# Re-dealing the steps of two low-rank MLPs around an eight-sequence encoder, inside one large single-core kernel

## The chip, the cores and the metric

The kernel runs on one core of a Trainium2 chip. Four engines matter here, each with its own queue that it works through in order: PE (TensorE, the matrix engine), DVE (VectorE), ACT (ScalarE) and POOL (GpSimd). A fifth queue, SP, issues most of the DMA transfers. The metric is the time of one execution on the device in microseconds (us), lower is better; the median of three executions is quoted.

## The reference, cut to what matters

The network adds eight sublayers to a residual stream `x` of shape (8, 256, 128), each on a layer-normed input. The first four are a linear recurrence, a low-rank-modulated MLP, a four-layer encoder, and the same MLP a second time:

```python
x = L0_attn_a_u
x = x + _L0_attn_a_ref(_layernorm(x, axis=-1), ...)      # recurrence
x = x + _L0_ffn_ref(_layernorm(x, axis=-1), ...)         # low-rank MLP, first time
x = x + _L0_attn_b_ref(_layernorm(x, axis=-1), ...)      # encoder, 4 layers
x = x + _L0_ffn_ref(_layernorm(x, axis=-1), ...)         # low-rank MLP, second time
x = x + _L1_attn_a_ref(_layernorm(x, axis=-1), ...)      # causal attention
...
```

The low-rank MLP and one encoder layer are these:

```python
def _L0_ffn_ref(x, W1, b1, W2, b2, scale):
    lt = x[:, 1:17]; even, odd = lt[:, ::2], lt[:, 1::2]
    m1 = (even[:, :4, :, None] * odd[:, :4, None, :]).reshape(Bx, Hx, Dx)
    m2 = (even[:, 4:, :, None] * odd[:, 4:, None, :]).reshape(Bx, Dx, Hx)
    h = einsum('bsd,hd->bsh', x, W1) + scale * einsum('bsd,bhd->bsh', x, m1) + b1
    h = gelu(h)
    return einsum('bsh,oh->bso', h, W2) + scale * einsum('bsh,boh->bso', h, m2) + b2

def _encoder_layer(x, ...):
    h = _layernorm(x); q, k, v = h @ Wq, h @ Wk, h @ Wv
    x = x + _linear_attention(q, k, v) @ Wo
    h = _layernorm(x)
    return x + relu(h @ W1 + b1) @ W2 + b2
```

(The kernel's program takes the shapes of a larger instance: 8 batches of 512 tokens, D = 128.)

## The kernel before

A batch of 512 tokens lies in SBUF as four tiles of 128 x 128. All work on a batch is a Python generator that is cut into *steps* by `yield`. `pieces` (line 35) deals such generators out in rounds: its list of *ages* is one round, and the slot of age `a` in round `now` advances generator `now - a` by one step. A generator therefore starts in an early round at its lowest age and ends at its highest. A slot that has no generator (at the start and the end) does nothing but still counts, so `pieces` can advance a second stream, `side`, at every `every`-th slot from round `first` on. `in_program_order` (line 65) then pins the instructions of PE, DVE, ACT and POOL to the order in which they were written: what is dealt first stands first in each engine's queue.

**The low-rank MLP** is `lora_steps` (line 331). Per batch, in the order of its steps: layer-norm statistics (L174, L175, L160 on DVE, then the power -1/2 on POOL, L161); the normed tile `z` (two quarters on DVE, L192, two on ACT, L188) and a bias added into `x` on POOL (L221); transposes on PE (L201) and four small row picks (L358), evacuated to `zt`; `left` and `e` on DVE (L364 to L375); two outer-product matmuls (L381) and `w1e`, `w2e` on DVE (L384, L385); the up matmuls (L391) with Gelu on ACT (L392), in two steps; the down matmuls (L399), in two steps, and the add into `x` (L224). The first MLP is followed by two steps of `encoder_input` (statistics; normed and scaled on ACT, L188, four instructions, with a POOL add, L424). The second one is preceded by two steps of `encoder_output` (statistics; four ACT instructions, L188, then three POOL operations on 128 x 512, L439 to L441).

**The encoder** is `encoder_block` (line 479). 32 generators (4 layers x 8 batches) of 15 steps go through 35 rounds (-1 to 33) of 15 slots. In the order of its steps: 0 statistics; 1 normed `hn`; 2 bias add on POOL (L221); 3 transposes (L201) and `zt` (L208); 4 key, value and query matmuls (L533, L536), `vx` copies (L538) and two exponentials (L542, L547) on ACT, `kb` and `kp` on DVE (L540, L543); 5 L553, then `qp`, `ks`, `kv` on DVE (L555 to L560); 6 L567, then `den`, `at` on DVE (L569 to L571); 7 transposes (L581) and the copy `att` (L583); 8 output projection (L475), add (L586), statistics; 9 `hn`; 10 transposes and `zt`; 11 and 12 up matmuls (L600) with Relu (L601), step 11 with a POOL bias add (L221); 13 and 14 down matmuls (L608) and the add (L613). Gelu and the exponential are in different ACT tables, so that ACT loads a table (1.28 us in the trace) whenever it goes from one to the other.

How the three are joined. At the front, `before` (line 2250) deals the recurrence, the first MLP beside it, and beside the last rounds of that MLP the encoder's first pieces: `side=take(side, 22), every=1, first=B - 2`, one encoder piece after each slot of the MLP's rounds 6 and 7, 22 in all, and none in its rounds 8 and 9. Two of the 22 are `filled()` (L496 to L502), which sets constants on POOL. At the back, one piece of the second MLP is dealt after each of the encoder's last twelve pieces; the rest runs after the encoder in a region of program order of its own, with a pool of its own (`lora`, two buffers of `mlp_g`). From its round 5 on, the four steps of `attention_input` (two layer norms of batch 0 and a transpose, for the causal attention) stand beside it.

Behind that, `attention_block` clears two tiles `strips0`, `strips1` on POOL (L680, L683), and the weights of the experts (`w_m`, 4.5 MB) are loaded by SP into the room of the encoder's weights once these are free.

Of the kernel before, what the change touches and what calls it, by code (L numbers as in the profile page):

```python
# [10 lines left out]
F32 = mybir.dt.float32  # L11
# [8 lines left out]
P = 128  # L20
B = 8
S = 512
# [14 lines left out]
def pieces(make, count, ages, side=None, every=0, first=0):  # L37

    live = {}
    done = 0
    starts = {start: n for n, start in enumerate(range(count) if isinstance(count, int) else count)}
    for now in range(min(ages), 1 + max(starts) + max(ages)):
        for age in ages:
            n = starts.get(now - age)
            if n is not None:
                if n not in live:
                    live[n] = make(n)  # L50
                next(live[n], None)
            done += 1
            if side is not None and now >= first and done % every == 0:
                next(side, None)
            if n is not None:
                yield
# [271 lines left out]
LORA_FIRST = (2, -2, 0, 1, -1, 0, 2, -1, 1, -1, -2)  # L328
LORA_SECOND = (-3, -2, 0, 1, -1, 0, -1, 1, -1, -2, -4)


def lora_steps(k, room, ahead=None, behind=None):

    nc = k.nc
    w, pool = k.packs["f"], k.work

    def steps(b):
        if ahead is not None:  # L340
            for _ in ahead(b):
                yield
        x = k.xb(b)
        found = k.norm_start(x)
        yield
        z = k.work.tile([P, NT, D], F32, name="z")
        k.norm_end(x, z, found, split=True)
        k.add_bias(x, k.row["f_b2"])
        yield

        zt = k.work.tile([P, S], F32, name="zt")
        k.flip(z, zt)


        pt = k.ps([P, 2, D], "b")
        for g in range(4):
            rows = slice(32 * (g % 2), 32 * (g % 2) + 4)
            nc.tensor.matmul(pt[rows, g // 2, :], w["pick"][0:32, g, :], z[0:32, 0, :], start=True, stop=True)  # L358
        yield
        left = pool.tile([P, D], F32, name="left", bufs=1)  # L360
        e = pool.tile([P, 4, D], F32, name="e", bufs=1)
        parts = [slice(32 * i, 32 * i + 4) for i in range(2)]
        for rows in parts:
            nc.vector.tensor_scalar(left[rows], pt[rows, 0, :], k.col["scale"][rows, :], None, ALU.mult)  # L364
        one, two = parts
        nc.vector.tensor_tensor(
            e[one],
            pt[one, 1:2, :].to_broadcast([4, 4, D]),
            k.ident[one, one, None].to_broadcast([4, 4, D]),
            ALU.mult,  # L370
        )
        e2 = e[two].rearrange("p c (i q) -> p c i q", i=4)
        ev = pt[two, 1, :].rearrange("p (q c) -> p c q", c=4)
        for i in range(4):
            nc.vector.tensor_scalar(e2[:, :, i, :], ev, k.ident[two, 32 + i : 33 + i], None, ALU.mult)  # L375
        yield
        w1 = pool.tile([P, 512], F32, name="w1e")
        w2 = pool.tile([P, 4, D], F32, name="w2e")
        p1, p2 = k.ps([P, 512]), k.ps([P, 4, D])
        for rows, to in ((one, p1), (two, p2.rearrange("p c o -> p (c o)"))):  # L380
            nc.tensor.matmul(  # L381
                to, left[rows], e[rows].rearrange("p i d -> p (i d)"), start=True, stop=True
            )
        nc.vector.tensor_tensor(w1, w["w1"], p1, ALU.add)  # L384
        nc.vector.tensor_tensor(w2, w["w2"], p2, ALU.add)  # L385
        yield

        g = room().tile([P, 4, S], F32, name="mlp_g")
        for c in range(4):
            ph = k.ps([P, S])  # L390
            nc.tensor.matmul(ph, w1[:, c * P : (c + 1) * P], zt, start=True, stop=True)  # L391
            nc.scalar.activation(g[:, c, :], ph, AF.Gelu, bias=k.col["f_b1"][:, c : c + 1])  # L392
            if c % 2:
                yield

        py = k.ps([P, NT, D], "c")
        for t in range(NT):
            for c in range(4):
                nc.tensor.matmul(  # L399
                    py[:, t, :], g[:, c, t * P : (t + 1) * P], w2[:, c, :], start=(c == 0), stop=(c == 3)  # L400
                )
            if t == 1:
                yield
        k.add_x(b, py)
        yield
        if behind is not None:
            for _ in behind(b):
                yield

    return steps  # L410


def encoder_input(k, xe):

    nc = k.nc

    def steps(b):
        xb = xe[:, b * NT : (b + 1) * NT, :]
        mean, rs = k.norm_start(k.xb(b))
        yield  # L420
        scaled = k.small.tile([P, NT], F32, name="ln_sc")
        nc.vector.tensor_scalar(scaled, rs, math.sqrt(D), None, ALU.mult)
        k.norm_end(k.xb(b), xb, (mean, scaled), split=2)
        nc.gpsimd.tensor_tensor(xb, xb, k.packs["e"]["pos"], ALU.add)  # L424
        yield

    return steps


def encoder_output(k, xe):  # L430

    nc = k.nc

    def steps(b):
        xb = xe[:, b * NT : (b + 1) * NT, :]
        found = k.norm_start(xb)
        yield
        k.norm_end(xb, xb, found, split=2)
        nc.gpsimd.tensor_tensor(xb, xb, k.lnf[:, 0:1, :].to_broadcast([P, NT, D]), ALU.mult)  # L439
        nc.gpsimd.tensor_tensor(xb, xb, k.lnf[:, 1:2, :].to_broadcast([P, NT, D]), ALU.add)  # L440
        nc.gpsimd.tensor_tensor(k.xb(b), k.xb(b), xb, ALU.add)  # L441
        yield

    return steps
# [34 lines left out]
def encoder_block(k, xe, before, behind):  # L479
# [3 lines left out]
    nc, tc = k.nc, k.tc  # L483
# [3 lines left out]
    with tc.tile_pool(name="enc1", bufs=1, reuse_waits="tile") as one, tc.tile_pool(name="enc", bufs=2, reuse_waits="tile") as pool:  # L487
# [134 lines left out]
        left = L * B * len(ages)  # L622
        own = chain(filled(), pieces(steps, L * B, ages))
        with in_program_order(tc):

            done = 0

            def counted():
                nonlocal done
                for _ in own:  # L630
                    done += 1
                    yield

            stream = counted()
            before(pool, stream)
            for _ in stream:
                if done > left + 2 - 12:
                    next(behind)


def attention_input(k, b, pool, to, **bufs):

    x = k.xb(b)
    found = k.norm_start(x)
    yield
    z = pool.tile([P, NT, D], F32, name="z", **bufs)
    k.norm_end(x, z, found)
    found = k.norm_start(z)
    yield
    hn = pool.tile([P, NT, D], F32, name="hn", **bufs)  # L650
    k.norm_end(z, hn, found)
    yield
    k.flip(hn, to, k.col["l_ln1s"], k.col["l_ln1b"])
    yield
# [367 lines left out]
class Experts:  # L1022
# [37 lines left out]
    def behind(self, made):  # L1060
        tc = self.k.tc
        for i in reversed(tc.nc.cur_bb.bb.instructions):
            if i.engine == mybir.EngineType.PE:
                tc.add_manual_dep(made.ins, i.name, SYNC, reason="not all of them at once")
                return
# [356 lines left out]
def run(stream):  # L1422
    for _ in stream:
        pass
# [16 lines left out]
def take(stream, many):  # L1441

    for _ in range(many):
        if next(stream, stream) is stream:
            return
        yield
# [749 lines left out]
def net_kernel(ctx: ExitStack, tc: tile.TileContext, drams, offsets, out):  # L2196
    nc = tc.nc
    k = Net(ctx, tc, drams, offsets)
    for b in range(B):
# [20 lines left out]
    room = rooms.enter_context(tc.tile_pool(name="moe1", bufs=1, side="right", reuse_waits="tile"))  # L2220
    p_l = own.enter_context(tc.tile_pool(name="w_l", bufs=1, side="right", reuse_waits="tile"))
    ready = p_l.tile([P, S], F32, name="zt0")
# [11 lines left out]
    slots = [blank_slots(k, one) for one in GROUPS]  # L2234
    k.load("l", p_l, parts=2)
    k.load("lrow", p_l, rows=P)
    second = []
    xe = w_e.enter_context(tc.tile_pool(name="xe", bufs=1, reuse_waits="tile")).tile([P, B * NT, D], F32, name="xe")
    behind = pieces(
        lora_steps(k, lambda: second[0], ahead=encoder_output(k, xe)),  # L2240
        B,
        LORA_SECOND,
        side=attention_input(k, 0, k.work, ready),
        every=2,
        first=5,
    )

    def before(pool, side):
        free = xe.rearrange("p t d -> p (t d)")[:, (B - 2) * S :]
        k.load("a", queue=nc.scalar, into=free)  # L2250
        first = lora_steps(k, lambda: pool, behind=encoder_input(k, xe))
        after = pieces(first, B, LORA_FIRST, side=take(side, 22), every=1, first=B - 2)
        pipeline(rotation_steps(k, pool, free), B, ROTATION, side=after, every=3, first=5)
        run(after)

    with k.banks(**usual):
        encoder_block(k, xe, before, behind)
        with tc.tile_pool(name="lora", bufs=2, reuse_waits="tile") as pool, in_program_order(tc):
            second.append(pool)
            run(behind)  # L2260
    w_e.close()
    late = ctx.enter_context(tc.tile_pool(name="w_m", bufs=1, reuse_waits="tile"))
    rest = ExitStack()
# [262 lines left out]
```

## Time and profile before

| what | value |
|---|---|
| median of three executions | 1931.11 us (1929.14 to 1938.34) |
| the profiled execution's own time | 1931.14 us |
| its span in the profile | 1929.4 us |
| PE busy | 1687.2 us, 87% |
| DVE busy | 1267.0 us, 66% |
| ACT busy | 987.6 us, 51% |
| POOL busy | 766.5 us, 40% |
| recurrence and first MLP | about 0 to 190 us |
| encoder | about 135 to 638 us |
| second MLP | about 610 to 729 us |
| causal attention, experts, gated attention, experts | 729 to 1929 us |

The span is the time from the first to the last instruction that the profiler recorded; the 1.7 us between it and the execution's time lie around it. A row of the timeline gives the start and the length of an instruction (or of a group of equal ones, x count), its engine and source line, what it writes and reads, and in brackets how long its engine had been idle before it and which instruction released it. A row of a table of windows gives for a stretch of the span its length and each engine's busy time (with the number of instructions), then the mean granted clock of PE as a share of the full one, and the DMA share and rate. PE's matmuls are pipelined, so lengths of neighbouring groups overlap a little.

### The profile page before, as it was taken

The page shows a single profiled execution, that of the slowest core. Times are in us where ns is not written, and L with a number is a line of the kernel's source. Part 1 is how long each engine was busy: PE and PEld are TensorE (multiplying, and loading weights), DVE is VectorE, ACT ScalarE, POOL GpSimd, SP SyncE. Part 2 cuts the span into 40 slices and gives each one's busy share as a digit, 9 for nine tenths or more (in the row PEclk, how much of TensorE's full clock was granted, in tenths as well). Part 3 has the DMA queues.
Part 4 walks back from the last instruction along what each step waited for, and adds up shares of the span by engine and source line. Part 5 has one row for each costly group of instructions (what it writes and reads, how often), then busy time and mean ns, then how long its engine had stood idle before and what let it go on. Part 6 is the DMA issues. An engine that isn't in the chain of part 4 may idle for free.

```text
span 1929.4 us, 30031 instructions
## 1 busy us (share of the span) xinstructions
PE 1687.2 (87%) x10169; PEld 1155.5 (60%) x10169; DVE 1267.0 (66%) x4092; ACT 987.6 (51%) x1805; POOL 766.5 (40%) x895
## 2 busy tenths in 40 slices
PE   6987999999997988999998977878897878788986
PEld 4655878888786554344444555655555635576664
DVE  8776888888887766666676455364746584565563
ACT  3345666666665434665665533446443544444553
POOL 4443333333334643444445825642212116145633
PEclk9998999999999999999998979989998677799998
DMA  9900000000000021000000111131001001112331
GB/s 256 179 1 1 1 1 1 1 1 1 1 1 1 1 96 45 1 1 1 1 1 15 52 39 55 50 108 32 13 8 40 12 3 38 42 41 63 107 110 58
DMA packets 79599, 71.33 MB, mean 37 GB/s; under 512 B 6560, under 2 KB 73376, under 8 KB 78544
## 3 DMA queue, kind: packets, MB, share of 16 engines
q1 hardware_dynamic: 69696, 49.67, 10.6%
q0 software_dynamic: 9312, 19.22, 3.1%
q8 instruction: 86, 1.41, 0.3%
q14 instruction: 73, 0.60, 0.1%
q10 hardware_dynamic: 432, 0.43, 0.1%
HBM read 35.05 MB, written 34.25 MB: 36 GB/s over the span
## 4 chain that ended last, share of the span: by engine, by line
PE 31%; DVE 14%; ACT 7%; issue 5%; POOL 1%; DMA 1%; another core or an unknown queue 0%; DVEq 0%; ACTq 0%; POOLq 0%; SPq 0%
PE ps_a L1360 4%; PE ps_a L1361 3%; PE ps_s L755 3%; PE ps_y L1333 3%; PE ps_b L1324 2%; PE ps_o L784 2%; DVE sh L1749 2%; PE ps_a L1767 2%; PE ps_c L975 1%; ACT pr L765 1%; PE ps_a L1333 1%; DVE x L1410 1%; DVE hid L1374 1%; DVE half L1373 1%; PE ps_b L1939 1%
## 5 line engine op out<-in xcount | busy, mean ns | idle before, releaser
L161 POOL TENSOR_TENSOR ln_rs<-rs_v,mhalf 128x4 f32<-128x4 f32 x144 | 149.0, 1035 | 348.5 <-DVE rs_v L160 338.2
L1257 POOL DMA_INDIRECT given<-yr,to x163 | 158.6, 973 | 280.0 <-PE ps_a L1360 81.3
L765 ACT ACTIVATE pr<-ps_s 128x1024 f32<-128x1024 f32 x160 | 154.7, 1019 | 123.2 <-PE ps_s L755 120.2
L1373 DVE SCALAR_TENSOR_TENSOR half<-half,ps_a 128x352 f32<-128x352 f32 x163 | 84.5, 519 | 197.7 <-ACT half L1366 158.7
L1245 POOL DMA_INDIRECT slots<-xn,rpos x128 | 125.8, 983 | 83.9 <-issue 33.6
L769 POOL TENSOR_SCALAR_AFFINE_SELECT pr<-pr 128x256 f32<-128x256 f32 x256 | 99.8, 415 | 108.6 <-ACT pr L765 104.7
L755 PE MATMUL ps_s<-qm,rot 32*128 32x128 f32 (+3 forms) x1024 | 123.6, 483 | 19.1 <-ACT pr L765 18.9
L1361 PE MATMUL ps_a<-w_m,xt 128*128 x326 | 131.7, 487 | 8.1 <-ACT yr L1336 7.6
L1360 PE MATMUL ps_a<-w_m,xt 128*128 x326 | 133.6, 493 | 5.7 <-ACT xt L1306 5.5
L1326 ACT COPY gt<-ps_b 128x384 f32<-128x384 f32 x163 | 78.1, 479 | 117.8 <-PE ps_b L1324 92.1
L608 PEld LDWEIGHTS ps_c<-w_e,mlp_g 128*128 128x128 f32 x1024 | 122.0, 192 | 17.0 <-issue 14.1
L608 PE MATMUL ps_c<-w_e,mlp_g 128*128 128x128 f32 x1024 | 125.0, 275 | 1.8 <-ACT mlp_g L601 1.7
L600 PE MATMUL ps_a<-zt,w_e 128*128 128x512 f32 x256 | 123.5, 606 | 3.3 <-ACT zt L208 3.3
L1366 ACT ACTIVATE half<-ps_a 128x352 f32<-128x352 f32 x163 | 76.0, 466 | 94.6 <-PE ps_a L1360 79.2
L175 DVE BATCH_NORM_AGGREGATE ln_mv<-ln_st 128x2 f32<-128x6 f32 x576 | 104.8, 182 | 19.9
L1324 PEld LDWEIGHTS ps_b<-w_ident,hid 128*128 128x128 f32 x489 | 62.9, 146 | 90.4 <-issue 31.3
L1324 PE MATMUL ps_b<-w_ident,hid 128*128 128x128 f32 x489 | 84.8, 284 | 35.5 <-DVE hid L1374 29.4
L601 ACT ACTIVATE mlp_g<-ps_a,w_col 128x512 f32<-128x512 f32 x128 | 87.4, 687 | 46.5 <-PE ps_a L600 46.5
L221 POOL TENSOR_TENSOR xe<-xe,w_erow 128x512 f32<-128x512 f32 x64 | 82.0, 1302 | 64.5 <-DVE ks L558 61.2
L755 PEld LDWEIGHTS ps_s<-qm,rot 32*128 32x128 f32 x1024 | 58.8, 191 | 77.8 <-ACT pr L765 52.0
L1374 DVE SCALAR_TENSOR_TENSOR hid<-half,ps_a 128x352 f32<-128x352 f32 x163 | 85.0, 521 | 21.1 <-PE ps_a L1361 3.1
L208 ACT ACTIVATE zt<-ps_b,w_col 128x512 f32<-128x512 f32 x80 | 62.7, 784 | 61.8 <-PE ps_b L201 61.8
(390 smaller groups left out, 3999.1 us busy)
## 6 DMA issues: line engine op xcount, KB each, us to landing
xr<-slots SPq DMA_DIRECT2D x37, 260.0 KB
y<-given SPq DMA_DIRECT2D x32, 256.0 KB
slots<-blank SPq DMA_DIRECT2D x3, 2535.0 KB
w_m<-in_m_dram SPq DMA_DIRECT2D x2, 2244.0 KB
w_e<-in_e_dram SPq DMA_DIRECT2D x2, 1700.0 KB
slots<-blank SPq DMA_DIRECT2D x2, 1495.0 KB
given<-yr,to POOLq DMA_INDIRECT x163
x<-in_u_dram SPq DMA_DIRECT2D x8, 256.0 KB
```

The source lines that it names most:

```text
L161: nc.gpsimd.tensor_tensor(out, v, self.mhalf[:, :n], ALU.pow)
L175: nc.vector.bn_aggr(mv[:, t, :], st[:, t, :])
L600: nc.tensor.matmul(ph, w1[:, c * P : (c + 1) * P], ht, start=True, stop=True)
L608: nc.tensor.matmul(py[:, t, :], g[:, c, t * P : (t + 1) * P], w2[:, c, :], start=(c == 0), stop=(c == 3))
L755: nc.tensor.matmul(halves[g // 2][:, g % 2, at : at + S - u * P], kr[rows, u * P : (u + 1) * P], qm[rows, i, u * P : S], start=True, stop= ...
L765: nc.scalar.activation(pr, sc, AF.Exp)
L1245: made = nc.gpsimd.indirect_dma_start(out=g.slots, out_offset=bass.IndirectOffsetOnAxis(ap=g.pos[:, i, t : t + 1], axis=0), in_=g.xn[:, t, :],
L1257: made = nc.gpsimd.indirect_dma_start(out=g.given, out_offset=bass.IndirectOffsetOnAxis(ap=to, axis=0), in_=yr, in_offset=None,)
L1324: nc.tensor.transpose(pt[:, q, :], hid[:, q, :], k.ident)
L1360: nc.tensor.matmul(pg, xt, w["experts"][:, bass.ds(o + HID, HID)], start=True, stop=True)
L1361: nc.tensor.matmul(pv, xt, w["experts"][:, bass.ds(o, HID)], start=True, stop=True)
L1374: nc.vector.scalar_tensor_tensor(flat, half, 0.5, pv, ALU.mult, ALU.mult)
```

## The change

Three things change. The second MLP draws `mlp_g` from the encoder's pool and is dealt wholly inside the encoder's region of program order. Its first 23 pieces stand in the encoder's last six rounds, by a table that is keyed by the number of encoder pieces still to come: one piece at 66, 59, 51, 44, 36, 29, 21, 16, 13 and at 10 to 4 to come, two at 3, 2 and 1, one at 0; then the rest follows in the same region. At the front the encoder's pieces are dealt after every second slot of the first MLP from round 5 on, with no limit of 22: that is 28 pieces in rounds 5 to 9.

```diff
-        g = room().tile([P, 4, S], F32, name="mlp_g")
+        g = room.tile([P, 4, S], F32, name="mlp_g")
...
+            after = behind(pool)
+            beside = dict.fromkeys((66, 59, 51, 44, 36, 29, 21, 16, 13, *range(4, 11)), 1)
+            beside.update({3: 2, 2: 2, 1: 2, 0: 1})
             stream = counted()
             before(pool, stream)
             for _ in stream:
-                if done > left + 2 - 12:
-                    next(behind)
+                for _ in range(beside.get(left + 2 - done, 0)):
+                    next(after)
+            run(after)
...
-    second = []
-    behind = pieces(
-        lora_steps(k, lambda: second[0], ahead=encoder_output(k, xe)),
-        B, LORA_SECOND, side=attention_input(k, 0, k.work, ready), every=2, first=5,
-    )
+    def behind(pool):
+        second = lora_steps(k, pool, ahead=encoder_output(k, xe))
+        side = attention_input(k, 0, k.work, ready)
+        return pieces(second, B, LORA_SECOND, side=side, every=2, first=5)
...
-        after = pieces(first, B, LORA_FIRST, side=take(side, 22), every=1, first=B - 2)
+        after = pieces(first, B, LORA_FIRST, side=side, every=2, first=B - 3)
...
         encoder_block(k, xe, before, behind)
-        with tc.tile_pool(name="lora", bufs=2, reuse_waits="tile") as pool, in_program_order(tc):
-            second.append(pool)
-            run(behind)
```

The two programs hold the same instructions on every engine. Their order on PE, DVE, ACT and POOL differs only in two stretches, around the start and around the end of the encoder; SP's queue is the same. One instruction group moves that the diff doesn't name: in the program before, POOL clears `strips0` and `strips1` behind the last work of the second MLP, `strips1` behind a wait for the MLP's last matmuls (its room was that of the `lora` pool); in the changed program both clearings stand in POOL's queue right behind the last power (L161) that follows the last L441, ahead of two L221 and three L161 of the second MLP's last batches and of `attention_input`.

## The prediction

> **What bounds the kernel now.** I read the page's slices first (PE's busy tenths and its granted clock), then windows cut at the encoder's two ends, then PE's timeline there, and last the queues of DVE, ACT and POOL behind each wait.
>
> ```profile
> PE   6987999999997988999998977878897878788986
> ...
> PEclk9998999999999999999998979989998677799998
> ```
>
> A slice is 48.2 us. From the fifth to the twelfth (193 to 579 us) PE is full: the encoder is bound by PE at full clock, and nothing can be won there. The change touches slices 3, 4 and 13 to 15, where PE is at 7 to 9 tenths.
>
> ```profile
> 122.08:189.40 67.32, 51.61 (x276) 36.79 (x277) 46.45 (x180) 34.88 (x68) 24.79 (x27) 0.92 0.00 1
> 568.94:582.86 13.92, 13.92 (x89) 11.20 (x88) 11.13 (x40) 8.92 (x19) 4.60 (x4) 1.00 0.00 1
> 605.49:649.69 44.20, 31.48 (x142) 18.07 (x141) 30.18 (x118) 20.22 (x40) 26.94 (x23) 0.85 0.00 1
> 649.69:698.28 48.59, 46.76 (x257) 29.61 (x255) 39.57 (x155) 22.93 (x47) 31.63 (x27) 0.96 0.14 53
> 698.28:729.36 31.08, 26.82 (x153) 19.83 (x153) 12.63 (x34) 9.01 (x13) 6.96 (x8) 0.89 0.16 68
> ```
>
> Columns: stretch, length, busy PE, weight load, DVE, ACT, POOL, clock, DMA. The first row is the front end (MLP round 5 to the end of PE's longest wait), with PE idle 15.7 us. The second is one encoder round: PE 13.92 of 13.92, but DVE also 11.13, so only 2.8 us of DVE are free in a round. The third is the back end, PE idle 12.7 us at a clock of 0.85.
>
> ```profile
> 141.77 0.66 PE L201 MATMUL ps_b<-w_ident,hn 128*128 128x128 f32 x4 [2.74 <-DVE zt L154]
> ...
> 172.03 2.26 PE L553 MATMUL ps_c<-vx,kp 128*128 128x144 f32 x8 [3.21 <-DVE kp L543]
> ...
> 189.40 2.07 PE L475 MATMUL ps_c<-w_e,att 128*128 128x128 f32 x8 [4.99 <-ACT att L583]
> ```
>
> The front waits for chains through DVE, POOL and ACT: the first `hn`, `kp` (a table load stands before it), and `att`, which stood in ACT's queue behind eight L188 of two encoder inputs.
>
> ```profile
> 612.65 3.74 PE L608 MATMUL ps_c<-w_e,mlp_g 128*128 128x128 f32 x28 [1.74 <-ACT mlp_g L601]
> 620.41 0.69 PE L201 MATMUL ps_b<-w_ident,hn 128*128 128x128 f32 x2 [4.02 <-DVE hn L192]
> 621.76 0.69 PE L201 MATMUL ps_b<-w_ident,hn 128*128 128x128 f32 x2 [0.66 <-DVE hn L192]
> 625.77 5.25 PE L600 MATMUL ps_a<-zt,w_e 128*128 128x512 f32 x8 [3.32 <-ACT zt L208]
> ...
> 639.71 3.37 PE L391 MATMUL ps_a<-zt,w1e 128*128 128x512 f32 x4 [2.90 <-DVE ln_mv L175]
> ```
>
> The back waits for the last sequence's second norm and for the MLP's first batch. After the 3.32 us wait eight L600 take 5.25 us; in a full round four take 1.88.
>
> **The change, front end.** No instruction is added, so the terms are waits only. Between 122.08 and 189.40 the brackets on PE's rows add up to 16.4 us (0.86, 0.87, 2.74, 2.04, 1.70, 3.21, 4.99), and rows behind them that ran slower than their equals in a full round lose 4.4 (L533 2.46 for 1.89, L536 1.91 for 1.02, L381 1.45 for 1.13, L567 and L553 2.26 for 1.25, L391 2.45 for 1.88). I walk the new order through the four queues with the durations of the rows. Round 5: DVE now does the encoder's first statistics (four pairs L174/L175 and L160, 1.8) by 128.4. POOL does its power only behind both fills (L496 to L499 2.0, L501 and L502 1.2) and two other powers, by 131.3. `hn` (0.75) and, queued behind it on DVE, `left` and `e` (2.5) then end at 134.7 instead of 129.5, and L391, behind `w1e`, starts at 136.8 instead of 132.41: 4.4 lost. Round 6: after five MLP groups L533 ends at 145.0 and L536 at 145.9; `vx` (0.62), the table load (1.28), `km` (0.91) and `kp` release L553 at 147.9, a wait of 2.0. `left`, `e`, `kv` and `w1e` of the last batch queue behind `kp` on DVE, two waits of 0.6, and two of 0.3 behind them. Rounds 7 and 8 are full but for 0.6 before the second L553. In round 9 `att` stands behind one encoder input instead of two: DVE has `den` and `at` (2.1), two statistics (3.6) and two small operations (0.4), then ACT four L188 (1.65) and `att` (0.57): L475 starts at 181.1, a wait of 4.4. That is 8.3 earlier than 189.40 at full clock. The waits that remain are fewer and further apart, so I give back a quarter of the 4.4, 1.1: **-7.2**. Ends: -12 if the fills on POOL lie beside waiting anyway, -2 if all 4.4 come back and one more DVE wait of 2 appears.
>
> The clock is the first place to weigh a rule. Here the granted clock fell to 0.76 behind waits of 2.74 and 2.04, and to 0.50 behind 4.99. The Trainium skill, "TensorE: Matmul & The Clock Gate", section "What's actually happening", says that the array falls to half rate after about one idle window of 3.4 us and needs as long at work to recover; the trace shows drops after shorter waits as well. By that page, as an estimate, each wait over 3.4 us costs 1.7 us: two such waits before, four after by my walk (4.4 twice here, two below), so the change would lose 3.4 to the clock where I let it gain, and the sum would be about 1928.
>
> **Back end.** From the first L600 of encoder round 32 (605.49) to the MLP's first L399 (649.69) PE does the same instructions in both orders, 25.5 us of starts at full clock. In the new order the first batch's transposes, L358 and L381 stand before the last `hn`, and L391 between the last L600. Walk: batch 1's statistics on DVE (1.8) make `at` and L581 1.6 late; L475 ends at +7.5; L586, statistics and L160 at +10.5; then the power (1.2) beside `w1e`, `w2e` (1.3) and `z` (0.75); `hn` and L201 at +13.9 (before +14.9). `zt` stands on ACT behind four L188 of batch 3, which need statistics (1.8), power (1.2) and 1.65: L600 at +19.4 (before +20.3). From there the order is dense: the 2.90 wait and slow L391 go, L399 starts at +34.8 instead of +44.2: -9.4 (ends -5 and -13, the whole idle time).
>
> What it costs earlier: seven pieces in full rounds 28 to 31. Statistics (1.8) fill DVE's wait for the first power (1.20 in each round) and overrun it by 0.5. The three POOL operations at 59 and 44 to come (3 x 1.27) start when four L188 end, and push two L221 (2.57) and the next round's power 1.5 late; `hn`, and behind it L586, statistics, `kb`, `kp`, come that much later, and L553 has about 0.2 to spare: 1.3 lost, twice. `z` at 29 to come delays `kv` by 0.8. Sum with round 28's 0.5: **+3.9** (ends 0, if POOL's work falls into gaps, and 8).
>
> The moved clearings cost too:
>
> ```profile
> 700.82 1.16 PE L201 MATMUL ps_b<-w_ident,hn 128*128 128x128 f32 x4 [2.53 <-DVE hn L192]
> ```
>
> ```profile
> 709.56 1.81 POOL L680 MEMSET strips<- 128x2048 f32 x1
> 711.42 0.57 POOL L683 MEMSET strips<- 128x256 f32 x2
> ```
>
> PE already waits 2.53 for `attention_input`, whose two powers are POOL's at 694.64 and 699.28. Two clearings, 4.8 us, now start at 692.04 and hold POOL until 696.85; the L221 and the first power follow at 698.1 to 699.1 instead of 694.64 to 695.66. The chain behind it is serial, so PE waits 5.5: **+3.0** (ends 0 and 4.8). What they did at 726 released nobody, so nothing is won there. DMA: SP's order and the release of `w_m`'s room (the last L441) stay; no term.
>
> The second rule is about POOL beside DVE:
>
> ```profile
> 619.04 2.66 DVE L192 TENSOR_SCALAR hn<-xe,ln_mv,ln_rs 128x128 f32<-128x128 f32 x2
> ```
>
> Two L192 take 0.60 elsewhere; here L439 and L440 ran on POOL. L560 likewise takes 1.05 in full rounds beside L221, 0.31 without. But L174 stayed at 0.26 to 0.29 beside L439 to L441, so I add nothing beyond the queueing. The Trainium skill, "SBUF — State Buffer", section "SBUF: two separate sides", has one port pair shared by DVE and GpSimd, locked for a whole instruction. By it, as an estimate, each moved POOL operation may hold up one DVE operation for its 1.27 us; for the nine of the first three groups the sum would be 11 higher.
>
> **Sum:** -7.2 - 9.4 + 3.9 + 3.0 = -9.7. From the profiled 1931.14 (span 1929.4 and 1.7 around it; the median is 1931.11) that gives 1921.4; I say **1921**.
>
> **Rivals.** (A) *The inserted pieces are hidden*, since they stand where DVE, ACT and POOL wait in a full round: stalls 0, clearing 1, front -10, back -9.4: 1913. For it: ACT has 1.77 idle where 1.65 of L188 go. Against: kp's 0.2 of slack. (B) *The back end gives everything back*: stalls 8, clearing 4.8, front -7.2: 1927.5. For it: DVE 11.13 + 2.6 of 13.92. (C) *Slower: POOL's added operations block DVE for their whole length*: four groups of three (15.3), two bias adds (2.5) and clearings (4.8), 22.6, against -9.4 and the front's poor end -2: 1942. It decides once the blocking passes 21 us. For it: the 2.66 row; against: L174 beside the same operations. (D) *The order does nothing*: the end stays PE's work; 1931. Against: the queues do change.
>
> **Numbers.** Forecast 0.50, A 0.24, B 0.10, C 0.12, D 0.04. 0.5% (9.7 us) is about what this measurement tells from no change: 1921.5 and 1940.8. The forecast, 1914 to 1928, lies half on each side: faster 0.25 + 0.24 = 0.49; same 0.25 + 0.10 + 0.04 = 0.39; slower 0.12. The range is **1907 to 1936**: A's with a front of -12 and a clearing of 0, and most of C left out.
>
> **What would show it.** Right: L475's wait near 181 and under 4.99; L381 about 4 late in round 5; L553 waiting about 1 in rounds 29 and 30; L399 at 640 to 645; the `hn` wait before the last L399 groups 4 to 6. Wrong: PE full in rounds 28 to 31 (A), or L192 and L570 stretched there (C).

## The result: no difference that this measurement shows, and the profile after

| | before | after |
|---|---|---|
| median | 1933.71 us (12 executions, 1921.34 to 1942.99) | 1933.06 us (12, 1920.57 to 1938.86) |
| ratio, 95% interval | | 0.9996 (0.9973 to 1.0020) |
| profiled execution | 1931.14 us, span 1929.4 | 1938.86 us, span 1937.1 |

The forecast was 1921, faster; the time lies within its range (1907 to 1936), the direction was not met. The profiled execution of after is the longest of its twelve, so its span can't be held against the other's; the stages must be compared one by one. From here on the program is cut at five PE rows into: *front* (the MLP's fifth-round L391, at 122.08 before, to the first waiting encoder L475), *encoder* (to the first L600 of encoder round 32, at 605.49 before, which belongs to the last sequence but one), *back* (to the second MLP's first L399), *second MLP* (to the first L475 of the attention) and *rest*. The first two fences are of the page of after (busy and clock by slices) and of its windows, cut at the front, one round of the encoder, the back and the second MLP; columns as before. The granted clock is always full or half; a "slow" row is one that ran, in whole or in part, at the half, and the last section has the evidence.

```profile
PE   7988999999998988999998877788797877888885
...
PEclk9898999999999988999998989989997678899998
```

```profile
124.38:189.39 65.01, 52.97 (x276) 36.79 (x276) 49.92 (x183) 35.46 (x68) 26.93 (x29) 0.91 0.00 1
568.60:584.03 15.43, 14.17 (x88) 11.23 (x87) 13.21 (x50) 10.34 (x21) 9.22 (x9) 1.00 0.00 1
608.08:643.55 35.47, 29.38 (x141) 17.27 (x141) 20.88 (x77) 15.33 (x26) 15.48 (x14) 0.90 0.00 0
643.55:731.91 88.36, 75.93 (x418) 50.55 (x416) 59.45 (x198) 31.71 (x59) 37.20 (x35) 0.94 0.19 77
```

The front is 2.3 shorter (67.32 before), at about the same clock (0.92 before); a late encoder round is 1.5 longer (13.92), with PE idle 1.26 of it; the back is 8.7 shorter (44.20). PE's timeline of after says where it still waits:

```profile
135.50 3.20 PE L381 MATMUL ps_a<-e,left 4*128 4x512 f32 x4 [2.71 <-DVE e L366]
...
152.37 1.44 PE L553 MATMUL ps_c<-vx,kp 128*128 128x144 f32 x8 [1.98 <-DVE kp L543]
153.60 3.41 PE L399 MATMUL ps_c<-w2e,mlp_g 128*128 128x128 f32 x16
...
175.25 1.22 PE L553 MATMUL ps_c<-vx,kp 128*128 128x144 f32 x8 [2.32 <-DVE kp L543]
...
189.39 2.08 PE L475 MATMUL ps_c<-w_e,att 128*128 128x128 f32 x8 [4.41 <-ACT att L583]
...
574.39 1.25 PE L553 MATMUL ps_c<-vx,kp 128*128 128x144 f32 x8 [1.26 <-DVE kp L543]
...
626.71 3.78 PE L600 MATMUL ps_a<-zt,w_e 128*128 128x512 f32 x4 [4.54 <-ACT zt L208]
...
695.65 1.15 PE L201 MATMUL ps_b<-w_ident,hn 128*128 128x128 f32 x4 [5.29 <-DVE hn L192]
```

The larger waits that the prediction named are there, and most have its size; the second L553 waits 2.32 where it said 0.6, and the four small waits that it saw behind the first L553 (two of 0.6, two of 0.3) are not in the trace. What it had not counted stands in the second column: L399 takes 3.41 where it takes 1.95 at full clock, L600 3.78 for 1.88, and L381 3.20 where four such rows take 1.13 in a full round (not all of this is the clock, as e7 will show).

### The profile page after: what moved, and what is told of

It reads as the page before. It is cut to its first block, busy times and chain, and to the rows that moved or that the text cites. A ratio compares the mean times of both kernels' runs of the same rounds, so it can differ in the third digit from the quotient of the medians.

```text
span 1937.1 us, 30016 instructions
## 1 busy us (share of the span) xinstructions
PE 1692.1 (87%) x10169; PEld 1158.9 (60%) x10169; DVE 1268.4 (65%) x4092; ACT 987.2 (51%) x1805; POOL 766.1 (40%) x895
## 4 chain that ended last, share of the span: by engine, by line
PE 31%; DVE 14%; ACT 7%; issue 4%; POOL 1%; DMA 1%; another core or an unknown queue 0%; DVEq 0%; SPq 0%; ACTq 0%; POOLq 0%
PE ps_a L1367 4%; PE ps_a L1366 4%; PE ps_s L761 3%; PE ps_y L1339 3%; PE ps_b L1330 2%; PE ps_o L790 2%; PE ps_c L981 2%; DVE sh L1755 2%; ACT pr L771 1%; PE ps_a L1773 1%; PE ps_a L1339 1%; DVE x L1416 1%; DVE hid L1380 1%; DVE half L1379 1%; PE ps_a L1924 1%
## 5 line engine op out<-in xcount | busy, mean ns | idle before, releaser
L161 POOL TENSOR_TENSOR ln_rs<-rs_v,mhalf 128x4 f32<-128x4 f32 x144 | 148.7, 1033 | 318.8 <-DVE rs_v L160 312.8
L1332 ACT COPY gt<-ps_b 128x384 f32<-128x384 f32 x163 | 78.0, 479 | 127.1 <-PE ps_b L1330 88.7
L608 PEld LDWEIGHTS ps_c<-w_e,mlp_g 128*128 128x128 f32 x1024 | 122.0, 192 | 16.3 <-issue 16.3
L600 PE MATMUL ps_a<-zt,w_e 128*128 128x512 f32 x256 | 124.5, 609 | 4.8 <-ACT zt L208 4.8
L608 PE MATMUL ps_c<-w_e,mlp_g 128*128 128x128 f32 x1024 | 124.7, 275 | 0.0
L221 POOL TENSOR_TENSOR xe<-xe,w_erow 128x512 f32<-128x512 f32 x64 | 81.8, 1297 | 55.5 <-DVE ks L558 52.7
L1367 PEld LDWEIGHTS ps_a<-w_m,xt 128*128 128x128 f32 x326 | 64.3, 201 | 50.0 <-ACT yr L1342 13.2
```

The source lines that it names most:

```text
L161: nc.gpsimd.tensor_tensor(out, v, self.mhalf[:, :n], ALU.pow)
L600: nc.tensor.matmul(ph, w1[:, c * P : (c + 1) * P], ht, start=True, stop=True)
L608: nc.tensor.matmul(py[:, t, :], g[:, c, t * P : (t + 1) * P], w2[:, c, :], start=(c == 0), stop=(c == 3))
L1367: nc.tensor.matmul(pv, xt, w["experts"][:, bass.ds(o, HID)], start=True, stop=True)
```

## The experiments

Ratios compare with the kernel before on the same chip. Chips differ in the rest (the kernel before has medians of 1937.9, 1900.6, 1934.1 and 1902.8 on the four of e1 to e16), not in the four stages, so the stages of all profiles can be set side by side (us):

| run | front | encoder | back | second MLP | sum | rest | ratio (95%) |
|---|---|---|---|---|---|---|---|
| before | 67.3 | 416.1 | 44.2 | 86.4 | 614.0 | 1193.4 | |
| after | 65.0 | 418.7 | 35.5 | 88.4 | 607.5 | 1205.2 | 0.9996 (0.9973 to 1.0020) |
| e1_front_alone | 66.1 | 415.4 | 44.5 | 86.4 | 612.4 | 1193.6 | 0.9997 (0.9974 to 1.0019) |
| e2_back_alone | 67.7 | 418.9 | 36.4 | 88.7 | 611.6 | 1192.1 | 0.9955 (0.9932 to 0.9978) |
| e3_after_again | 65.1 | 418.8 | 35.5 | 88.4 | 607.7 | 1201.5 | 0.9971 (0.9950 to 0.9991) |
| e4_strips_behind | 64.9 | 419.4 | 35.8 | 85.4 | 605.5 | 1204.8 | 0.9961 (0.9942 to 0.9980) |
| e5_pool_gap | 66.1 | 429.7 | 37.6 | 86.9 | 620.3 | 1169.4 | 1.0043 (1.0027 to 1.0059) |
| e6_fills_early | 62.2 | 418.9 | 35.6 | 86.8 | 603.4 | 1167.6 | 0.9985 (0.9975 to 0.9996) |
| e7_warm | 61.9 | 421.3 | 33.3 | 85.3 | 601.9 | 1168.6 | 0.9988 (0.9974 to 1.0002) |
| e8_three_mends | 62.8 | 427.4 | 36.4 | 83.8 | 610.4 | 1171.3 | 1.0003 (0.9993 to 1.0012) |
| e9_act_gap | 65.2 | 424.8 | 35.9 | 86.9 | 612.8 | 1200.1 | 1.0058 (1.0034 to 1.0083) |
| e10_all_mends | 63.0 | 424.1 | 33.3 | 82.5 | 602.9 | 1197.3 | 0.9943 (0.9922 to 0.9964) |
| e11_after_third | 65.0 | 417.7 | 37.5 | 86.9 | 607.1 | 1200.8 | 0.9985 (0.9969 to 1.0001) |
| e12_before_again | 67.7 | 415.7 | 44.4 | 82.0 | 609.8 | 1195.9 | |
| e13_mends_dealt | 62.2 | 416.4 | 35.0 | 82.5 | 596.1 | 1175.2 | 0.9931 (0.9905 to 0.9957) |
| e14_back_mended | 67.2 | 418.9 | 33.3 | 81.7 | 601.0 | 1164.6 | 0.9969 (0.9951 to 0.9987) |
| e15_before_third | 67.7 | 415.7 | 44.4 | 82.1 | 609.9 | 1168.2 | |
| e16_after_fourth | 65.0 | 418.7 | 35.5 | 88.4 | 607.5 | 1166.1 | 0.9993 (0.9980 to 1.0005) |

**One junction at a time.** The kernel before with the front's line alone, and the changed kernel with that line put back:

```diff
-        after = pieces(first, B, LORA_FIRST, side=take(side, 22), every=1, first=B - 2)   # e1: this, in before
+        after = pieces(first, B, LORA_FIRST, side=side, every=2, first=B - 3)             # e2: the reverse, in after
```

> Only the front junction is changed (the encoder's first pieces one round earlier and every second place); the back is the kernel before. Stages, each from one PE row to the next: front = the fifth-round L391 at 122.08 to the first encoder L475 (67.3 before, 65.0 after); encoder = to the first L600 of the last sequence (416.1, 418.7); back = to the second MLP's first L399 (44.2, 35.5); second MLP = to the first attention L475 (86.4, 88.4); rest (1193.4, 1205.2). Theory (the clock's half-rate windows come back behind the waits that remain): front 64 to 66.5, that is 1 to 3 gained and not 7, the other stages as before, time within 3 of before. Rival A (my walk holds, and the profile of after was an unlucky execution): front 59 to 61.5. Rival B (the order does nothing): 67.

> Only the back junction is changed; the front is the kernel before. Theory (the terms add up one by one): front 67 to 68, encoder 418.5 to 419.5 (two waits of 1.3 before L553), back 35 to 36, second MLP 88 to 89 with the wait of 5.3 before the last norm's transposes; net -3 to -5, time ratio 0.997 to 0.999. Rival (the back's gain needs the new front): back over 40.

e1: the front falls by 1.2 and no other stage by more than 0.7, within the bounds of the theory; the walk of 7 falls, and with it the rival by which the profile of after was an unlucky execution. e2: the stages are those of after with the old front, so by stages the two junctions are independent. Its net, -2.4, misses the -3 to -5 that was expected, while its ratio, 0.9955, lies under the 0.997 expected and under what its stages give (611.6 against 614.0 is 0.9988); nothing in its profile explains that.

**The same kernel again, beside the kernel before.**

> The changed kernel once more, nothing else. Theory (what follows the first attention matmul differs by execution and not by the change): the four stages up to there within 1.5 each of 65.0, 418.7, 35.5 and 88.4, but the rest 1190 to 1200 and not 1205. Rival (the change costs 12 in the stages behind it, in which the order is the same): the rest 1203 to 1207 again.

> The changed kernel once more, beside the kernel before on the same chip. Theory (front 2.3, back 8.7 gained; encoder 2.6, second MLP 2.0 lost; nothing behind): the four stages sum to 607.5 within 1.5, ratio 0.9955 to 0.998. Rival (something behind the first attention matmul gives part of it back): the stages as said, ratio over 0.9985, and the rest longer than that of the kernel before in e12 by over 3.

> The kernel before, profiled on the same chip as e9 to e11. Theory: four stages of 67.3, 416.1, 44.2 and 86.4 within 1 each; its rest within 3 of the rest in e9, e10 and e11. Rival: its rest is over 3 shorter than theirs.

> The kernel before, for its stages beside e16. Theory: sum of the four stages 610 to 614, the rest within 4 of that of e16. Rival (the change lengthens what follows): the rest over 4 shorter than e16's.

> The changed kernel, beside e15 on the same chip. Theory: sum of the four stages 606.5 to 608, the rest within 4 of e15's, ratio 0.9965 to 0.999. Rival: the rest over 4 longer than e15's, ratio 0.999 to 1.001.

The stages of the changed kernel repeat to within 2 of each other in four profiles. The rest does not: 1205, 1202, 1201 on chips where the kernel before had 1193 and 1196, which looked like a loss of 5 to 12 behind the change; but on the chip of e15 and e16 it is 1168.2 before and 1166.1 after. So no loss behind is shown, and none is excluded on the other chips: e3 missed its bound of 1200, e11 is on its rival's side (4.9 longer than e12, with a ratio of 0.9985, just at the rival's bound), and e12 missed its own bound of 3 against e9 and e11. What makes the rest move by 5 to 12 where the order is the same stays open. The four ratios of the changed kernel, each weighted by the inverse square of its interval, give 0.9988 plus or minus 0.0008, some 2.4 us faster, and the stages of e15 and e16 say the same: 609.9 - 607.5 = 2.4. (e16's ratio, 0.9993, is in its rival's bounds although its rest is not longer; its stages alone give 0.9987, inside its interval.)

The kernel before gave a surprise of its own: its second MLP takes 86.4 in two profiles (before, e1) and 82.0 in two (e12, e15). PE's timeline of e12:

```profile
690.05 2.55 PE L391 MATMUL ps_a<-zt,w1e 128*128 128x512 f32 x4 [0.23 <-DVE w1e L384]
692.39 3.05 PE L399 MATMUL ps_c<-w2e,mlp_g 128*128 128x128 f32 x16
...
699.19 1.01 PE L201 MATMUL ps_b<-w_ident,hn 128*128 128x128 f32 x4 [0.87 <-DVE hn L192]
```

A slow step of the clock fell on L391 and L399 ahead of the wait for `hn`; PE came later, waited 0.87 instead of 2.53, and no slow step followed the wait; in e15 it is the same (0.88), and in before and e1 a slow step follows a wait of 2.5. In the changed kernel the wait is 5.3, and in all four profiles a slow step lies on the rows behind it.

**The clearings.** The changed kernel, with POOL's clearings held behind its last norm:

```diff
+        k.last_pool = [i.name for i in tc.nc.cur_bb.bb.instructions if i.engine == mybir.EngineType.Pool][-1]
...
+            for i in nc.cur_bb.bb.instructions[first:]:
+                if strips and i.engine == mybir.EngineType.Pool:
+                    tc.add_manual_dep(i, k.last_pool, ORDER, reason="behind the norms")
```

> The changed kernel, with the two strips' clearings held behind POOL's last instruction of the encoder's region, where the kernel before had them. Theory (the clearings hold POOL 4.8 before the last norm's power): the wait before the last norm's four L201 falls from 5.29 to 2.3 to 2.8, the second MLP's stage from 88.4 to 85.5 to 86.5. Rival (another wait takes its place): the wait falls but the stage stays over 87.5, for the first attention matmul waits for the clearings or for the same norm by another way.

```profile
691.66 1.15 PE L201 MATMUL ps_b<-w_ident,hn 128*128 128x128 f32 x4 [2.52 <-DVE hn L192]
```

The wait falls from 5.29 to 2.52 and the stage by 2.9: the clearings' price in the changed order, and no wait takes its place. It is not the clock's luck: PE is idle 9.65 in this stage instead of 12.43.

**The dealt pieces.** First the two pieces that hold ACT's four L188 and POOL's L439 to L441 six places later, then three places earlier:

```diff
-            beside = dict.fromkeys((66, 59, 51, 44, 36, 29, 21, 16, 13, *range(4, 11)), 1)
+            beside = dict.fromkeys((66, 53, 51, 38, 36, 29, 21, 16, 13, *range(4, 11)), 1)   # e5
+            beside = dict.fromkeys((66, 62, 51, 47, 36, 29, 21, 16, 13, *range(4, 11)), 1)   # e9
```

> The changed kernel, with two of the dealt pieces (those with ACT's four L188 and POOL's L439 to L441) six places later, so that POOL has them behind the two L221 of the round and not in front. Theory (the three POOL operations push the L221 and the next power, and kp with them): the two waits of 1.26 before L553 vanish and the encoder stage falls from 418.7 to 415.8 to 416.8, all other stages unchanged. Rival (the pieces cost their time wherever they stand, since DVE is short of room): another wait of 1 to 1.5 per round appears and the encoder stays over 418.

> The changed kernel, with the same two dealt pieces three places earlier instead of later: ACT's four L188 (1.65) then stand in its idle 1.90 before km, POOL's order is unchanged. Theory (POOL stands at L439 until ACT has done the four L188, and everything behind it on POOL is late): L439 starts 3 earlier, the waits of 1.26 before L553 go, encoder 415.9 to 416.8 instead of 418.7, all other stages unchanged. Rival (it is the 3.8 of work on POOL, wherever it starts): the waits before L553 stay over 0.8 and the encoder over 417.7.

Both theories fell: the encoder became 11.0 and 6.1 longer than in the changed kernel. The rivals' bounds on the encoder hold, but neither gives the reason. PE is idle 5.0 and 2.5 longer in that stage than in the changed kernel; the rest of the loss is matmuls at the half clock. The timeline of e5, of POOL, DVE and PE:

```profile
566.44 1.28 POOL L439 TENSOR_TENSOR xe<-xe,lnf 128x512 f32<-128x512 f32 x1 [4.22 <-ACT xe L188]
...
571.42 0.16 DVE L185 SCALAR_TENSOR_TENSOR ln_nm<-ln_mv,ln_rs 128x4 f32<-128x4 f32 x1 [3.68 <-POOL ln_rs L161]
...
576.00 2.29 PE L553 MATMUL ps_c<-vx,kp 128*128 128x144 f32 x8 [3.59 <-DVE kp L543]
```

POOL stood 4.22 at L439 until ACT had done its four L188; the next round's power stood behind it, DVE waited 3.68 for that power, `kp` came late and PE waited 3.59 instead of 1.26, after which the clock fell. In e9 the four L188 came early enough, and it is the timeline of DVE, POOL and PE that shows the price:

```profile
555.65 0.76 DVE L540 TENSOR_TENSOR kb<-ps_a,bk 128x256 f32<-128x256 f32 x2 [1.97 <-ACT vx L538]
556.65 1.84 DVE L543 SCALAR_TENSOR_TENSOR kp<-km,kb 128x256 f32<-128x256 f32 x2 [0.24 <-ACT km L542]
...
556.78 1.42 POOL L440 TENSOR_TENSOR xe<-xe,lnf 128x512 f32<-128x512 f32 x1
...
557.13 0.76 PE L553 MATMUL ps_c<-vx,kp 128*128 128x144 f32 x4 [2.13 <-DVE kp L543]
```

On ACT the L188 now stood ahead of `vx`, and DVE's `kb` waited 1.97 for `vx`; then the two L543 took 1.84 instead of 0.82, ending 0.3 behind the L440 (556.78 to 558.20) that ran beside them. The Trainium skill, "SBUF — State Buffer", section "SBUF: two separate sides", describes the port pair that DVE and GpSimd share as an exclusive lock for the whole instruction; these two rows agree with it. A piece is a place in three queues at once, and of the three placements tried the change's was the cheapest: 2.6 over the encoder of before.

**The fills.** The changed kernel, with `filled()` one MLP round earlier, in a gap of 3.17 on POOL:

```diff
+        held.append(chain(idle(2), side))
+        def filling(b):
+            own = inputs(b)          # encoder_input
+            next(own)
+            yield
+            if b == 2:
+                next(side), next(side)
+            yield from own
-        after = pieces(first, B, LORA_FIRST, side=side, every=2, first=B - 3)
+        after = pieces(first, B, LORA_FIRST, side=held[0], every=2, first=B - 3)
```

> The changed kernel, with POOL's two fills (L496 to L502, 3.2 together) one MLP round earlier, in a gap of 3.17 of POOL between a power and L424; the order on PE, DVE and ACT is the same. Theory (the fills make POOL's power late and with it hn, left and e): the wait of 2.71 before L381 falls below 1, its slow rows go, front 60.5 to 63.5 instead of 65.0. Rival (the fills lay beside waiting anyway, and the wait moves on to kp and L553): front 64 to 65.5.

```profile
131.16 2.25 PE L381 MATMUL ps_a<-e,left 4*128 4x512 f32 x4 [1.27 <-ACT hn L188]
```

L381 starts 9.68 behind its L391 instead of 11.12, with a wait of 1.27 (now for ACT) instead of 2.71, and the front falls by 2.8 to 62.2, inside the theory's bounds, though the wait did not go below 1. Half of the 2.8 is the earlier start (1.44), the other half comes from L381 and L201 at full clock. The change's own fills on POOL cost it about half of what its front could have gained.

**The clock.** Transposes of the identity into a PSUM tile that nothing reads, on PE in front of its waits; they add work and change no result:

```diff
+def warm(k, n):
+    pt = k.ps([P, NT, P])
+    for t in range(n):
+        k.nc.tensor.transpose(pt[:, t % NT, :], k.ident, k.ident)
...
+            if i == L * B - 1:       # before L600 of the last sequence; likewise before three other rows
+                warm(k, 28)
```

> The changed kernel, with 100 transposes of the identity into PSUM that nothing reads, on PE in front of five waits: 16 before L381 (wait 2.71), 24 before the first L475 (4.41), 28 before L600 of the last sequence (4.54), 32 before the last norm's L201 (5.29). Theory (a wait of about 2 or more within one step of the clock brings the half rate, and the rows behind it cost the gain): the rows behind them run at full clock (L381 1.13 instead of 3.20, L475 1.15 instead of 2.08, L600 1.9 instead of 3.78, L391 1.96 instead of 2.79); front 61 to 63.5, back 33.5 to 35, second MLP 87 to 88, 4 to 7 less in all. Rival (the clock drops for another reason, or the chains through DVE and ACT set the end there and not PE): the rows are quicker but the stages stay within 0.7 of 65.0, 35.5 and 88.4; or the added work makes them longer.

```profile
129.65 2.25 PE L383 MATMUL ps_a<-e,left 4*128 4x512 f32 x4 [0.96 <-DVE e L366]
132.33 1.88 PE L393 MATMUL ps_a<-zt,w1e 128*128 128x512 f32 x4
...
620.40 1.98 PE L606 MATMUL ps_a<-zt,w_e 128*128 128x512 f32 x4 [1.49 <-ACT zt L208]
```

These are L381, L391 and L600 of after. The first starts 11.12 behind the front's beginning, as in after, so only what follows is quicker. It takes 2.25 at full clock and not the 1.13 that was expected: DVE writes the two halves of `e` one after the other (L366, then 1.13 of L375), and while PE waits for `e` the second half of L381 starts 1.16 behind the first, where both start together in a full round. So of the 3.20 in after only 0.95 is the clock. L600 takes 1.98 instead of 3.78, the back falls from 35.5 to 33.3 and the second MLP from 88.4 to 85.3; the front falls by 3.1. The 24 before L475 stood one sequence too late, where PE does not wait: the 4.40 stays, and the encoder is 2.6 longer, their full price (24 took 2.78). So the slow rows behind these waits cost the change 3.1, 2.2 and 3.1 in the three stages, the last two more than was expected, and transposes are free only where PE waits.

**Together.** e8 and e10 hold the strips, the fills and (e10) 102 transposes with the dealt pieces moved as in e5 and e9; e13 is e10 with the pieces where the change has them; e14 has the old front and, of the rest, the strips and 42 transposes at the back:

```diff
+            if i < 2:                # e10, e13: before the first two L553
+                warm(k, 14)
...
+            if i == 1:               # e10, e13: before the L475 that waits
+                warm(k, 24)
```

> The changed kernel with three mends together: the strips' clearings behind POOL's last norm, the two POOL pieces six places later, the fills one round earlier. Theory (the terms add up): front 60.5 to 63.5, encoder 415.8 to 416.8, back 35 to 36, second MLP 85.4; 12 to 16 under the kernel before up to the first attention matmul, time ratio 0.991 to 0.995. Rival (what is gained ahead is lost in the stages behind, whose length moves by execution and arrival): the four stages fall as said but the ratio stays over 0.996.

> The changed kernel with all mends: strips' clearings behind the last norm, fills one round earlier, ACT's four L188 in their gap, and 102 transposes that nothing reads before six waits of PE (8 before L381, 14 before each of the first two L553, 24 before the first waiting L475, 28 before the last sequence's L600, 14 before the last norm's L201). Theory (each term by itself): front 57.5 to 60.5, encoder 415.9 to 416.8, back 33 to 34, second MLP 82 to 84.5: 20 to 25 under the kernel before up to the first attention matmul; ratio 0.987 to 0.991. Rival (part of it is lost behind, as in the runs so far): the stages fall as said and the ratio is 0.992 to 0.997.

> The kernel of e10 with the dealt pieces where the changed kernel has them. Theory (each term by itself, from the stages of e10 and of the changed kernel): front 62 to 63.5, encoder 418 to 419.5, back 33 to 34, second MLP 82 to 83; sum 596 to 600 against 610 to 614 of the kernel before, ratio 0.990 to 0.995. Rival (what is gained before the first attention matmul is lost behind it): the stages as said and a ratio over 0.996.

> The kernel of e2 (back junction alone, the front as before), with the strips' clearings behind the last norm and the transposes that nothing reads before the last sequence's L600 (28) and the last norm's L201 (14). Theory: front 67 to 68, encoder 418 to 419.5, back 33 to 35, second MLP 82 to 84; sum 601 to 605, ratio 0.994 to 0.997, that is 4 to 6 behind e13. Rival (the front's terms do not reach the end): within 2 of e13.

In e8 and e10 the moved pieces cost 9 and 5 in the encoder and hide the rest, and both miss the ratios that were expected. The two mends of the front do not add: it is 62.2 with the early fills, 61.9 with the transposes, and 63.0 with both in e10, where 57.5 to 60.5 was expected. e13, whose theory took this over, meets its sum, 596.1; its back is 1 longer than said, with a slow L600 (3.66), and its encoder 1.6 shorter, as the slow L475 and L533 at its beginning are gone. PE's timeline of e13:

```profile
183.78 1.16 PE L477 MATMUL ps_c<-w_e,att 128*128 128x128 f32 x8 [1.81 <-ACT att L587]
...
620.49 1.98 PE L608 MATMUL ps_a<-zt,w_e 128*128 128x512 f32 x4 [1.48 <-ACT zt L208]
...
684.52 1.00 PE L201 MATMUL ps_b<-w_ident,hn 128*128 128x128 f32 x4 [0.99 <-DVE hn L192]
```

These three rows run at full clock (its L477 and L608 are L475 and L600 of after), where after has 2.08, 3.78 and 1.15. At 0.9931 (0.9905 to 0.9957) it beats the kernel before by some 13 us and, on that chip, the median of the changed one (1899.93) by 9: the lowest ratio here. e14 is 6 behind it, as the front's terms said: they do reach the end.

## Why the prediction was wrong

**The front: -7.2 said, -2.3 found (-2.7 between e15 and e16). This is the step that failed, and in it the size of one term.** Slow rows cost the kernel before 4.4. The prediction gave back only "a quarter of the 4.4", 1.1, because fewer waits remain, and so let the change win 3.3 of clock. The rows say that nothing was won. Behind its waits L381 loses 0.95 to the clock, its L201 0.5, L391 1.6 and L399 1.46: 4.6 before the L475, where 1.1 was said. By the clock's record the front has 12.3 us of half rate, against 11.0 before. That is 3.5 of the 4.9 by which the stage missed, and e7 shows it: with PE kept busy ahead of L381 the first three rows run at full clock and 3.1 come back.

A second term was mis-sized too: the second L553 waits 2.32 where 0.6 was said, 1.7 more. Against it stand errors the other way. L381 comes 2.8 late where about 4 was said (e6 shows that the fills on POOL make it late), and the four small waits, 1.8 together, did not come. By position, the first L553 starts 28.0 behind the stage's beginning (25.8 said), and the L475 37.0 behind that L553 (33.2 said). Of these last 3.8 the slow L399 and the second L553 explain 3.2; what took the place of the small waits is not resolved.

**The encoder: +3.9 said, +2.6 to +3.0 found.** Rounds 29 and 30 wait 1.26 each (1.3 said); round 28 lost 0.26 (0.5), and the 0.8 for `kv` is not there. The mechanism is the one said: the three POOL operations start when ACT's four L188 end, for which POOL stands 3.71 at L439. What each such stand costs when a piece is moved, e5 and e9 show.

**The back: -9.4 said, -8.7 to -8.9 found.** L399 comes 35.5 behind the first L600 (34.8 said). The near hit has some luck in it: the slow rows behind the 4.54 before L600 cost 2.2, which e7 took off and the walk had not counted, and that L600 came at +18.6 where the walk had +19.4.

**The clearings: +3.0 said; the wait is 5.29 (5.5 said), and e4 gets back 2.9.** Right as a mechanism. But the second MLP of before, against which it counts, is 86.4 in the profiled execution and 82.0 in two later ones, so the stage lost 2.0 or 6.3. The prediction took one execution's waits and slow rows for the kernel's, and had no term for this.

The sum with these sizes is -2.7 + 3.0 - 8.9 + 6.3 = -2.3, a quarter of the -9.7 forecast, and under what one such measurement tells from no change.

**The rivals:** D (nothing changes) gave the right time for a wrong reason: four stages moved by 2 to 9 and nearly cancel. B put the giving back in the stalls and the clearing; the stalls were not worse than said, and most of the giving back is clock and the baseline of the second MLP. A fell with the two waits of 1.26. C fell: L192 and L570 keep their 0.60 (for two) and 0.35 in those rounds, though e9 has one row of what C supposed. Two of the prediction's sums are off: B's terms give 1927.3, not 1927.5, and the range's lower end, A's with -12 and 0, is 1910 and not 1907.

## What to carry to other kernels

A shorter or earlier wait is worth its length only if the matmuls behind it run at full clock. So cost each remaining wait of 2 us or more with the slow rows that follow it (2.2 to 3.1 us a stage here), and do not count on winning these back where the change leaves waits of that length. A piece that is dealt into a full round holds a place in each queue it uses; look for what each queue's head will stand and wait for, and not only for busy time. And where a stage's length depends on the clock, take the baseline from several executions.

## What the runs showed of the hardware

The granted clock has two values, full and half, and changes only at steps of 3.41 us, whose place against the program differs from execution to execution. These are windows of after, cut at its steps:

```profile
132.83:136.24 3.41, 0.74 (x2) 0.29 (x2) 2.80 (x10) 2.01 (x6) 2.60 (x3) 0.99 0.00 0
136.24:139.65 3.41, 3.41 (x8) 1.52 (x8) 2.47 (x7) 0.12 (x1) 0.39 (x1) 0.50 0.02 5
...
173.78:177.19 3.41, 1.89 (x13) 1.48 (x14) 3.00 (x11) 2.82 (x6) 1.01 (x1) 1.00 0.00 0
177.19:180.60 3.41, 3.12 (x26) 2.90 (x26) 2.11 (x8) 2.31 (x5) 0.83 (x1) 1.00 0.00 0
```

In the first step PE was idle 2.7 of 3.41 and the next is at 0.50. The wait of 2.32 before the second L553 is split by a step's edge, so that its step was idle 1.5, and the clock stayed. Over the 18 profiles, of the steps at full clock up to 1860 us in which PE was idle over 2.0 us, 406 of 406 were followed by half rate, and no step idle over 1.98 was followed by a full one; less idle is no safety, as 341 more steps, with less idle than that, were followed by half rate too, and what decides there is open. The Trainium skill, "TensorE: Matmul & The Clock Gate", section "What's actually happening", has the free-running window of 3.4 us; it asks for an idle window, and here 2.0 idle of 3.41 were enough every time. The prediction weighed that page and set it aside on the sum: by it, as an estimate, the change was to lose 3.4 to the clock and end at 1928, which was nearer.
